# Two attention layers on a graph, fp32: the dense products by one level of Strassen's algorithm

## The chip, the cores and the metric

The kernel runs on one core of a Trainium2 chip, as one launch. The metric is device time in microseconds (us). The engines of the core work side by side, each through its own queue of instructions in order: TensorE (PE in the profile; its weight loads are listed apart as PEld), VectorE (DVE), ScalarE (ACT), GpSimd (POOL), and SyncE (SP), which here only starts transfers.

## The reference

64 graphs of 256 nodes with 512 features pass through two layers of masked attention, each before a residual sum. All arithmetic is fp32.

```python
h = jnp.maximum(_layernorm(x), 0.0)                 # layer 0: 4 heads of 64
q, k, v = h @ Wq, h @ Wk, h @ Wv                    # 512 -> 256
attn = softmax(where(adj, q @ k.T * scale, -max))
x = x + (attn @ v) @ Wo + bo                        # 256 -> 512
h = jnp.maximum(_layernorm(x), 0.0)                 # layer 1: 8 heads of 64
h = layernorm(h) * gamma + beta                     # its own norm on top
q, k, v = split(h @ w_qkv.T)                        # 512 -> 3 x 512
attn = softmax(where(adj | eye, q @ k.T * scale, -1e9))
x = x + (attn @ v) @ w_out.T + b_out                # 512 -> 512
```

## The kernel before, in words

A **step** handles two graphs (G = 2), so 512 tokens; there are 32 steps. Activations of a step lie in SBUF twice: with tokens in the 128 partitions (`xt`, `h`, `v`: four token tiles of 128) and with features in the partitions (`hT`, `oT`: chunks of 128 features by 512 tokens).

Per step and layer the work is:

- **Norm.** Statistics of a token tile on VectorE (`moments`, L140 and L141), the power -1/2 on GpSimd (L145), the scaling of `h` on VectorE (L160 in layer 0, L192 in layer 1). In layer 1 (`norm1_stats`) two norms stand behind each other: centering with the lower bound 0 (L177), statistics again. GpSimd adds the output bias into `xt` (L165 for layer 0, L182 for layer 1).
- **Transposes of h** (`transpose_h`, L204), four chunks; ScalarE (layer 0, with the lower bound 0) or VectorE (layer 1, with gamma and beta) takes them out of PSUM into `hT`.
- **q and k** (`project_qk`): for each pair of heads `pr` (2 pairs in layer 0, 4 in layer 1) and each of q and k, four matmuls of 128 features by 512 tokens (L223); ScalarE copies the result out (L227).
- **V** (`project_v`): for each token tile four matmuls, 256 columns wide in layer 0 and 512 in layer 1 (L235).
- **Attention per pair of heads**: `scores` (called S below: 8 matmuls, L267; then for each of eight 128x256 blocks one VectorE pass with mask and minimum, L276, and one exponential with its sum on ScalarE, L281; then the reciprocal L287 and the multiplication L290 on VectorE), `turn` (T: 16 transposes on TensorE, L304, copied out half by VectorE, L309, half by ScalarE, L311) and `weigh` (W: 8 matmuls with V, L323, copied into `oT` by ScalarE, L328).
- **Output product** (`combine`): for each token tile two (layer 0) or four (layer 1) matmuls of 512 columns (L245); VectorE adds the result into `xt` (L249).

An fp32 matmul appears in the profile as two records, each with its own weight load; a transpose as one.

**What sets the order.** Every call is an event with a time on a nominal clock (`at(period, place, ...)`), and the events are issued sorted by it. Three steps overlap: in one period the kernel does layer 1 of step s, layer 0's attention of step s+1 and layer 0's q, k and V of step s+2. TensorE's order is the written order (`manual_schedule` at L59); the other engines' orders are laid out by the framework's scheduler at build time and are fixed then. PSUM is cut into four buffers for scores and turns (`ps_sc`) and four for everything else (`ps_mm`, the tile name `mm`).

Of the kernel before, what the change touches and what calls it, by code (L numbers as in the profile page):

```python
# [9 lines left out]
U8 = mybir.dt.uint8  # L10
# [9 lines left out]
def kernel(  # L20
# [32 lines left out]
    io = ctx.enter_context(tc.tile_pool(name="io", bufs=3))  # L53
# [20 lines left out]
    wqkv0 = const.tile([P, NC, 3, I0], FP, name="wqkv0")  # L74
    wo0 = const.tile([P, PR0, D], FP, name="wo0")
# [3 lines left out]
    wqkv1 = const.tile([P, NC, 3 * I1], FP, name="wqkv1")  # L79
    wo1 = const.tile([P, PR1, D], FP, name="wo1")  # L80

    def first_weights():
        for k, w in enumerate((wq, wk, wv)):
            nc.scalar.dma_start(wqkv0[:, :, k, :], w.rearrange("(c p) o -> p c o", p=P))
        nc.scalar.dma_start(wo0, wo.rearrange("(c p) o -> p c o", p=P))
        for v, t in ((bo, bo_b), (b_out, bout_b)):
            nc.scalar.dma_start(t, bass.AP(tensor=v.tensor, offset=v.offset, ap=[[0, P], [1, D]]))
# [9 lines left out]
    def weight_loads():  # L97

        blocks = []
        tags = ("h1", "hT1", "qT1", "kT1")  # L100
        for src, dst in ((w_qkv, wqkv1), (w_out, wo1)):
            for r0 in range(0, src.shape[0] // P, 4):
                wr = act.tile([P, 4, src.shape[1]], FP, name="wr", tag=tags[len(blocks)])
                nc.scalar.dma_start(wr, src[r0 * P:(r0 + 4) * P].rearrange("(r p) i -> p r i", p=P))
                blocks.append((wr, dst, r0))
        return blocks

    def weight_block(wr, dst, r0, c):
        pw = ps_mm.tile([P, 4 * P], FP, name="mm")
        for r in range(4):  # L110
            nc.tensor.transpose(pw[:, r * P:(r + 1) * P], wr[:, r, c * P:(c + 1) * P], ident)  # L111
        nc.vector.tensor_copy(dst[:, c, r0 * P:(r0 + 4) * P], pw)
# [4 lines left out]
    def load(s):  # L117
        xt = io.tile([P, NT, D], FP, name="xt", bufs=4)
        nc.sync.dma_start(xt, x[s * G:(s + 1) * G].rearrange("g (t p) d -> p (g t) d", p=P))
        ad = io.tile([P, NT, N], U8, name="ad")  # L120
        nc.sync.dma_start(ad, adj[s * G:(s + 1) * G].rearrange("g (t p) j -> p (g t) j", p=P))
        S[s].update(xt=xt, ad=ad)

    def mask0(s):
        n0 = act.tile([P, NT, N], FP, name="n0")
        nc.gpsimd.tensor_scalar(n0, S[s]["ad"], -1.0, BIG, op0=ALU.add, op1=ALU.mult)
        S[s]["n0"] = n0

    def mask1(s):
        n1 = act.tile([P, NT, N], FP, name="n1")  # L130
        nc.gpsimd.tensor_scalar(n1, S[s]["ad"], -1.0, BIG, op0=ALU.add, op1=ALU.mult)
        for g in range(G):
            v = n1[:, g * NIC:(g + 1) * NIC, :]
            nc.gpsimd.tensor_tensor(v, v, offdiag, ALU.mult)
        S[s]["n1"] = n1
# [12 lines left out]
    def norm0_stats(s):  # L148
        mv = stat.tile([P, NT, 2], FP, name="mv0", bufs=2)
        for t in range(NT):  # L150
            moments(mv, S[s]["xt"], t)
        ve = stat.tile([P, NT], FP, name="ve0", bufs=2)
        nc.vector.tensor_scalar(ve, mv[:, :, 1], EPS, None, op0=ALU.add)
        S[s].update(mv=mv, r=rsqrt(ve, "r0"))

    def norm0_apply(s):
        xt, mv, r = S[s]["xt"], S[s]["mv"], S[s]["r"]
        h = act.tile([P, NT, D], FP, name="h0")
        for t in range(NT):
            nc.vector.tensor_scalar(  # L160
                h[:, t, :], xt[:, t, :], mv[:, t, 0:1], r[:, t:t + 1],
                op0=ALU.subtract, op1=ALU.mult,
            )
        for t in range(NT):
            nc.gpsimd.tensor_tensor(xt[:, t, :], xt[:, t, :], bo_b, ALU.add)  # L165
        S[s]["h"] = h
# [3 lines left out]
    def norm1_stats(s, t):  # L170
        st, x1 = S[s], S[s]["xt"]
        if t == 0:
            st["mv"] = stat.tile([P, NT, 2], FP, name="mv1", bufs=2)
            st["mg"] = stat.tile([P, NT, 2], FP, name="mg", bufs=2)
            st["h"] = act.tile([P, NT, D], FP, name="h1")
        moments(st["mv"], x1, t)
        nc.vector.tensor_scalar(  # L177
            st["h"][:, t, :], x1[:, t, :], st["mv"][:, t, 0:1], 0.0,
            op0=ALU.subtract, op1=ALU.max,
        )  # L180
        moments(st["mg"], st["h"], t)
        nc.gpsimd.tensor_tensor(x1[:, t, :], x1[:, t, :], bout_b, ALU.add)  # L182
        if t == NT - 1:
            ve = stat.tile([P, NT], FP, name="ve1", bufs=2)
            nc.vector.tensor_scalar(ve, st["mv"][:, :, 1], EPS, EPS, op0=ALU.add, op1=ALU.mult)
            nc.vector.tensor_tensor(ve, ve, st["mg"][:, :, 1], ALU.add)
            st["r"] = rsqrt(ve, "r1")

    def norm1_apply(s):
        st = S[s]  # L190
        for t in range(NT):
            nc.vector.tensor_scalar(  # L192
                st["h"][:, t, :], st["h"][:, t, :], st["mg"][:, t, 0:1], st["r"][:, t:t + 1],
                op0=ALU.subtract, op1=ALU.mult,
            )


    def transpose_h(s, lyr, c):
        st = S[s]
        if c == 0:  # L200
            st["hT"] = act.tile([P, NC, T], FP, name=f"hT{lyr}")
        ph = ps_mm.tile([P, T], FP, name="mm")
        for t in range(NT):
            nc.tensor.transpose(ph[:, t * P:(t + 1) * P], st["h"][:, t, c * P:(c + 1) * P], ident)  # L204
        if lyr == 0:
            nc.scalar.activation(st["hT"][:, c, :], ph, AF.Relu)  # L206
        else:
            nc.vector.tensor_scalar(
                st["hT"][:, c, :], ph, gb[:, 0, c:c + 1], gb[:, 1, c:c + 1],
                op0=ALU.mult, op1=ALU.add,  # L210
            )

    def weight(lyr, c, k):
        return wqkv0[:, c, k, :] if lyr == 0 else wqkv1[:, c, k * I1:(k + 1) * I1]

    def project_qk(s, lyr, pr, k):
        st, pairs = S[s], (PR0, PR1)[lyr]
        key = f"{'qk'[k]}T{lyr}"
        if pr == 0:
            st[key] = act.tile([P, pairs, T], FP, name=key)  # L220
        pp = ps_mm.tile([P, T], FP, name="mm")
        for c in range(NC):
            nc.tensor.matmul(  # L223
                pp, weight(lyr, c, k)[:, pr * P:(pr + 1) * P], st["hT"][:, c, :],
                start=(c == 0), stop=(c == NC - 1),
            )
        nc.scalar.copy(st[key][:, pr, :], pp)  # L227

    def project_v(s, lyr, t):
        st, inner = S[s], (I0, I1)[lyr]  # L230
        if t == 0:
            st[f"v{lyr}"] = act.tile([P, NT, inner], FP, name=f"v{lyr}")
        pv = ps_mm.tile([P, T], FP, name="mm")
        for c in range(NC):
            nc.tensor.matmul(  # L235
                pv[:, :inner], st["hT"][:, c, t * P:(t + 1) * P], weight(lyr, c, 2),
                start=(c == 0), stop=(c == NC - 1),
            )
        nc.scalar.copy(st[f"v{lyr}"][:, t, :], pv[:, :inner])  # L239

    def combine(s, lyr, t):
# [192 lines left out]
```

## Time and profile before

| | |
|---|---|
| median of 3 runs (lowest to highest) | 3934.84 us (3934.14 to 3936.08) |
| the profiled execution, time / span | 3935.06 / 3933.3 us |
| granted TensorE clock, mean | 0.998 |
| one step (distance of the same product in two steps) | 121.1 us |
| matmul records on TensorE | 16961 |
| GpSimd busy | 554.5 us, 14% of the span |
| HBM traffic over the span | 20 GB/s |

How to read the profile: the first part gives each engine's busy time and its share of the span. The chain that ended last is followed back from the last instruction, at each step to what released it; it tells whose work sets the end. The groups give, for one line, engine, operation and shape: the count, the busy time and the mean duration in ns of one instruction, then how long the engine stood idle just before them and who ended that. Records of one engine overlap, so the pace of a series is read from starts in the timeline, whose columns are start, time covered, engine, line, operation, shape and count. The waits list who waited for whom: total, times, longest. The table by stretches gives per engine the busy time and the number of instructions, then the granted clock, the share of the DMA engines and GB/s.

### The profile page before, as it was taken

What the parts mean: (1) busy time and instruction counts of PE and PEld (TensorE: products, weight loads), DVE (VectorE), ACT (ScalarE), POOL (GpSimd) and SP (SyncE); (2) the same over time, 40 slices, a digit from 0 to 9 for tenths busy, and PEclk for the clock granted to TensorE, in tenths of its full rate; (3) what the DMA queues carried; (4) which work ended last, traced back from release to release, by engine and by line L of the source; (5) the groups of instructions that cost most, each with busy time, mean ns of one, the idle gap of its engine ahead of it and who ended that gap; (6) DMA issues with size and microseconds to landing.
All of it is one profiled execution on the core that took longest, in us unless ns stands there. A gap on an engine that the chain in (4) does not pass through costs nothing.

```text
span 3933.3 us, 46557 instructions
## 1 busy us (share of the span) xinstructions
PE 3876.5 (99%) x16961; PEld 2178.9 (55%) x16961; DVE 2186.6 (56%) x7025; ACT 1503.9 (38%) x4417; POOL 554.5 (14%) x458
## 2 busy tenths in 40 slices
PE   7999999999999999999999999999999999999999
PEld 4555555555555555555555555555555555555554
DVE  5554655546555456555465554655545655556553
ACT  2434343333343343433434334334334343343333
POOL 3111111011111011111111101111101111111000
PEclk9999999999999999999999999999999999999999
DMA  3000000000000000000000000000000000000000
GB/s 118 1 23 23 23 2 24 22 23 24 2 23 22 23 23 17 9 22 24 23 24 2 23 22 23 24 2 23 22 23 23 13 13 22 23 24 11 1 11 22
DMA packets 55190, 81.10 MB, mean 21 GB/s; under 512 B 18088, under 2 KB 19632, under 8 KB 54960
## 3 DMA queue, kind: packets, MB, share of 16 engines
q1 hardware_dynamic: 50688, 71.31, 5.4%
q10 hardware_dynamic: 4272, 6.82, 0.5%
q8 instruction: 133, 2.18, 0.2%
q14 instruction: 97, 0.79, 0.1%
HBM read 44.57 MB, written 33.55 MB: 20 GB/s over the span
## 4 chain that ended last, share of the span: by engine, by line
PE 98%; ACT 1%; DVE 1%; DMA 0%; issue 0%; ACTq 0%
PE mm L223 34%; PE mm L235 17%; PE mm L245 17%; PE sc L267 9%; PE mm L323 9%; PE sc L304 9%; PE mm L204 3%; ACT kT L227 0%; DMA bout_b<-in_L_gnn_b_out_dram 0%; DVE pm L290 0%; PE mm L111 0%; ACT pm L281 0%; DVE pm L276 0%; DMA xt<-in_x_dram 0%; DVE pT L309 0%
## 5 line engine op out<-in xcount | busy, mean ns | idle before, releaser
L223 PE MATMUL mm<-hT,wqkv 128*128 128x512 f32 x3072 | 1369.2, 595 | 3.3 <-ACT hT L206 3.3
L276 DVE CUSTOM_DVE_ANT_0 pm<-sc,n 128x256 f32<-128x256 f32 x1536 | 544.6, 420 | 989.4 <-PE sc L267 985.7
L223 PEld LDWEIGHTS mm<-hT,wqkv 128*128 128x128 f32 x3072 | 567.2, 190 | 659.5 <-issue 620.7
L281 ACT ACTIVATE pm<-pm,sa 128x256 f32<-128x256 f32 x1536 | 758.5, 495 | 435.6 <-DVE sa L276 435.6
L235 PE MATMUL mm<-wqkv,hT 128*128 128x256 f32 (+1 forms) x2048 | 684.5, 487 | 0.0
L245 PE MATMUL mm<-wo,oT 128*128 128x512 f32 x1536 | 683.3, 594 | 0.0
L290 DVE TENSOR_SCALAR pm<-pm,sa 128x256 f32<-128x256 f32 x1536 | 555.0, 424 | 12.3
L235 PEld LDWEIGHTS mm<-wqkv,hT 128*128 128x128 f32 x2048 | 381.7, 190 | 265.6 <-issue 242.3
L245 PEld LDWEIGHTS mm<-wo,oT 128*128 128x128 f32 x1536 | 281.9, 190 | 319.4 <-issue 311.5
L309 DVE COPY pT<-sc 128x512 f32<-128x512 f32 x384 | 261.1, 687 | 299.2 <-PE sc L304 298.9
L267 PE MATMUL sc<-kT,qT 64*128 64x256 f32 x3072 | 385.6, 390 | 21.6 <-ACT kT L227 21.6
L304 PEld LDWEIGHTS sc<-ident,pm 128*128 128x128 f32 x3072 | 347.6, 142 | 87.2 <-issue 65.3
L304 PE MATMUL sc<-ident,pm 128*128 128x128 f32 x3072 | 372.3, 274 | 12.1 <-DVE pm L290 12.1
L267 PEld LDWEIGHTS sc<-kT,qT 64*128 64x128 f32 x3072 | 282.4, 187 | 179.5 <-issue 105.1
L182 POOL TENSOR_TENSOR xt<-xt,bout_b 128x512 f32<-128x512 f32 x128 | 162.5, 1270 | 1546.0 <-DVE h L177 1507.0
L323 PE MATMUL mm<-pT,v 128*64 128x256 f32 x3072 | 374.5, 386 | 0.0
L227 ACT COPY qT<-mm 128x512 f32<-128x512 f32 x192 | 112.6, 586 | 680.7 <-PE mm L223 680.7
L311 ACT COPY pT<-sc 128x512 f32<-128x512 f32 x384 | 225.2, 586 | 327.0 <-PE sc L304 327.0
L249 DVE TENSOR_TENSOR xt<-mm,xt 128x512 f32<-128x512 f32 x256 | 175.2, 685 | 287.3 <-PE mm L245 287.3
L239 ACT COPY v<-mm 128x256 f32<-128x256 f32 (+1 forms) x256 | 122.6, 479 | 473.7 <-PE mm L235 473.7
L281 ACT ACTIVATION_READ_ACCUMULATOR pm<-pm,sa 128x1 f32 x1536 | 286.4, 186 | 0.0
L227 ACT COPY kT<-mm 128x512 f32<-128x512 f32 x192 | 112.5, 586 | 454.0 <-PE mm L223 454.0
(40 smaller groups left out, 1942.1 us busy)
## 6 DMA issues: line engine op xcount, KB each, us to landing
xt<-in_x_dram SPq DMA_DIRECT2D x32, 1024.0 KB, 5.5
out_dram<-xt SPq DMA_DIRECT2D x32, 1024.0 KB, 4.3
ad<-in_adj_dram SPq DMA_DIRECT2D x32, 128.0 KB, 2.2
wr<-in_L_gnn_w_qkv_dram ACTq DMA_DIRECT2D x3, 1024.0 KB, 13.9
wr<-in_L_gnn_w_out_dram ACTq DMA_DIRECT2D x1, 1024.0 KB, 16.7
wqkv<-in_L_gnn_Wq_dram ACTq DMA_DIRECT2D x1, 512.0 KB, 7.0
wqkv<-in_L_gnn_Wk_dram ACTq DMA_DIRECT2D x1, 512.0 KB
wqkv<-in_L_gnn_Wv_dram ACTq DMA_DIRECT2D x1, 512.0 KB, 12.2
```

The costliest lines, as they stand in the source:

```text
L223: nc.tensor.matmul(pp, weight(lyr, c, k)[:, pr * P:(pr + 1) * P], st["hT"][:, c, :], start=(c == 0), stop=(c == NC - 1),)
L227: nc.scalar.copy(st[key][:, pr, :], pp)
L235: nc.tensor.matmul(pv[:, :inner], st["hT"][:, c, t * P:(t + 1) * P], weight(lyr, c, 2), start=(c == 0), stop=(c == NC - 1),)
L245: nc.tensor.matmul(po[:, :D], st[f"oT{lyr}"][:, pr, t * P:(t + 1) * P], w[:, pr, :], start=(pr == 0), stop=(pr == pairs - 1),)
L267: nc.tensor.matmul(sc[g, e][:, ic, :], qT[rows, pr, i0:i0 + P], kT[rows, pr, g * N:(g + 1) * N], start=True, stop=True,)
L276: nc.vector.tensor_tensor_reduce(out=pm[:, g, e, ic, :], in0=sc[g, e][:, ic, :], in1=neg[:, g * NIC + ic, :], scale=-SCALE, scalar=SMAX, o ...
L281: nc.scalar.activation(pm[:, g, e, ic, :], pm[:, g, e, ic, :], AF.Exp, bias=sa[:, 0, g, e, ic:ic + 1], scale=-1.0, accum_out=sa[:, 1, g, e ...
L290: nc.vector.tensor_scalar(pm[:, g, e, ic, :], pm[:, g, e, ic, :], sa[:, 2, g, e, ic:ic + 1], None, op0=ALU.mult,)
L304: nc.tensor.transpose(pp[:, jc, ic * P:(ic + 1) * P], pm[:, g, e, ic, jc * P:(jc + 1) * P], ident,)
L309: nc.vector.tensor_copy(pT[:, g, e], pp)
L311: nc.scalar.copy(pT[:, g, e], pp)
L323: nc.tensor.matmul(po[e * DH:(e + 1) * DH, g * N:(g + 1) * N], st[f"v{lyr}"][:, g * NIC + jc, c0:c0 + DH], pT[:, g, e, jc, :], start=(jc = ...
```

## The change

Strassen's algorithm multiplies two matrices, each cut into 2 x 2 blocks, with seven block products where the plain way needs eight. The changed kernel applies it (in Winograd's form, with fewer sums) once to each dense product.

- **Blocks.** The features are one cut (halves of the 512 inputs), the two graphs of the step the other. So `hT` and `oT` become tiles of seven blocks [128, 7, chunks, 256 tokens]: four of data, written by the evacuation to the places `B_OF`, and the others made from them by four subtractions on GpSimd (`act_sums`, L94 on), in a chain where most sums need one before. The weights become seven blocks likewise (`weight_sums`, once at the start).
- **Products.** They are issued in the order 1, 6, 7, 5, 2, 4, 3. Products 1, 6, 7 and 5 take a PSUM buffer each; 2, 4 and 3 accumulate onto the buffers of 1, 7 and 5, after those have been read. Product 1 needs data blocks only; product 6 needs the third sum of the chain, 7 the first, 5 the second, 4 the fourth.
- **Sums of results.** For q, k and V (`evacuate`): products 1 and 2 are copied by ScalarE, the other five are added by VectorE to what an earlier product has left in SBUF. For the output product (`accumulate`): VectorE adds six of the seven, GpSimd adds the block u = 1 + 6 into three blocks of `xt`.
- **Shapes.** A product of q and k serves two pairs of heads (one set in layer 0, two in layer 1): 4 matmuls of 256 columns. V has 4 matmuls per product, of 256 columns in layer 1 and 128 in layer 0. The output product has 4 (layer 1) or 2 (layer 0), of 256 columns.
- **Softmax.** The multiplication by the reciprocal moves from VectorE to GpSimd (L407). The turned block goes back into the tile it came from, so `pT` is gone.
- **Norm and loads.** `h` is loaded directly, normed in place and shared by both layers; x is loaded a second time for the residual (`load_x`), with the bias of layer 0 added by GpSimd (L180). `xt` has 2 buffers in place of 4. `norm1` is one event after layer 0's output product.
- **Order.** The nominal clock now counts sets of seven products. A period is: q/k of layer 1, first half; V of layer 1; q/k, second half; layer 0's output product of the next step; q/k of layer 0 and V of layer 0 for the step after that; layer 1's output product. S, T and W of the six pairs are set between them.

The core of the diff (`evacuate`, `accumulate` and the events in full, the rest cut):

```diff
+    A_OF = {(0, 0): 0, (0, 1): 1, (1, 1): 2, (1, 0): 3}
+    B_OF = ((0, 4, 3), (1, 3, 1))
+    PRODUCT = {1: (0, 0), 2: (1, 1), 3: (6, 2), 4: (2, 6), 5: (3, 3), 6: (4, 4), 7: (5, 5)}
...
+    def act_sums(b):
+        eng = nc.gpsimd
+        eng.tensor_tensor(b[:, 5], b[:, 2], b[:, 3], ALU.subtract)
+        eng.tensor_tensor(b[:, 3], b[:, 3], b[:, 0], ALU.subtract)
+        eng.tensor_tensor(b[:, 4], b[:, 2], b[:, 3], ALU.subtract)
+        eng.tensor_tensor(b[:, 6], b[:, 1], b[:, 4], ALU.subtract)
...
+    def norm1(s):
...
+        h = st["h"] = act.tile([P, NT, D], FP, name="h")
+        for t in range(NT):
+            moments(mv, x1, t)
+            nc.vector.tensor_scalar(
+                h[:, t, :], x1[:, t, :], mv[:, t, 0:1], 0.0, op0=ALU.subtract, op1=ALU.max
+            )
+            moments(mg, h, t)
+            nc.gpsimd.tensor_tensor(x1[:, t, :], x1[:, t, :], bout_b, ALU.add)
...
+        scale_rows(h, mg, rsqrt(ve, "r1"))
...
+    def evacuate(n, bank, region):
+        r11, r12, r21, r22 = region
+        add = nc.vector.tensor_tensor
+        if n == 1:
+            nc.scalar.copy(r21, bank)
+        elif n == 6:
+            add(r12, bank, r21, ALU.add)
+        elif n == 7:
+            add(r22, bank, r12, ALU.add)
+        elif n == 5:
+            add(r22, bank, r22, ALU.add)
+        elif n == 2:
+            nc.scalar.copy(r11, bank)
+        elif n == 4:
+            add(r21, bank, r12, ALU.add)
+        else:
+            add(r12, bank, r12, ALU.add)
+
+    def accumulate(n, bank, region, u):
+        r11, r12, r21, r22 = region
+        add = nc.vector.tensor_tensor
+        if n == 1:
+            nc.scalar.copy(u, bank)
+        elif n == 6:
+            add(u, bank, u, ALU.add)
+            nc.gpsimd.tensor_tensor(r12, r12, u, ALU.add)
+            nc.gpsimd.tensor_tensor(r21, r21, u, ALU.add)
+        elif n == 7:
+            add(r22, bank, r22, ALU.add)
+        elif n == 5:
+            add(r22, bank, r22, ALU.add)
+            nc.gpsimd.tensor_tensor(r22, r22, u, ALU.add)
...
+    SHARED = {2: 1, 4: 7, 3: 5}
...
     def project_qk(s, lyr, a, n):
...
+        bank, first = bank_of(st, ("qk", a), n, N)
+        wa, ba = PRODUCT[n]
+        for k in range(2):
+            for c in range(HC):
+                nc.tensor.matmul(
+                    bank[:, k, :], w[:, wa, c, k, a * P:(a + 1) * P], st["hT"][:, ba, c, :],
...
+        evacuate(n, bank, (t0[:, :, :N], t0[:, :, N:], t1[:, :, :N], t1[:, :, N:]))
...
-                    nc.vector.tensor_scalar(
-                        pm[:, g, e, ic, :], pm[:, g, e, ic, :], sa[:, 2, g, e, ic:ic + 1], None,
+                    nc.gpsimd.tensor_scalar(
+                        pm[g, e][:, ic, :], pm[g, e][:, ic, :], sa[:, 2, g, e, ic:ic + 1], None,
...
+    PROD = 1.75
+    SET = 7 * PROD
+    PERIOD = 6 * SET
...
+    def at_set(period, place, share, fn, *args):
+        for i, n in enumerate((1, 6, 7, 5, 2, 4, 3)):
+            at(period, place + i * share / 7, fn, *args, n)
...
+        at(p - 1, 5.6, load_h, s)
+        at(p, 1.0, norm0, s)
+        at(p, 2.9, mask, s, 0)
+        for c in range(NC):
+            at(p, 3.03 + 0.03 * c, transpose_h, s, 0, c)
+        at_set(p, 3.5, 1.0, project_qk, s, 0, 0)
+        at_set(p, 4.5, 0.5, project_v, s, 0)
+        at(p, 4.5, scores, s, 0, 0)
+        at(p, 5.15, turn, s, 0, 0)
+        at(p, 5.6, scores, s, 0, 1)
+        at(p, 5.601, weigh, s, 0, 0, True, False)
+        at(p, 6.3, turn, s, 0, 1)
+        at(p, 7.001, weigh, s, 0, 1, False, True)
+        at(p, 7.5, load_x, s)
+        at_set(p, 9.0, 0.5, combine, s, 0)
+        at(p, 9.5, norm1, s)
...
+        for c in range(NC):
+            at(p, -0.85 + 0.15 * c, transpose_h, s, 1, c)
+        at(p, 0.3, mask, s, 1)
+        at_set(p, 0.0, 1.0, project_qk, s, 1, 0)
+        at_set(p, 1.0, 1.0, project_v, s, 1)
+        at_set(p, 2.0, 1.0, project_qk, s, 1, 1)
+        at(p, 1.0, scores, s, 1, 0)
+        at(p, 1.65, turn, s, 1, 0)
+        at(p, 2.0, scores, s, 1, 2)
+        at(p, 2.001, weigh, s, 1, 0, True, False)
+        at(p, 2.65, turn, s, 1, 2)
+        at(p, 3.0, scores, s, 1, 1)
+        at(p, 3.001, weigh, s, 1, 2, False, False)
+        at(p, 3.5, turn, s, 1, 1)
+        at(p, 3.75, scores, s, 1, 3)
+        at(p, 3.751, weigh, s, 1, 1, False, False)
+        at(p, 4.25, turn, s, 1, 3)
+        at(p, 4.501, weigh, s, 1, 3, False, True)
+        at_set(p, 5.0, 1.0, combine, s, 1)
+        at(p, 6.0, store, s)
```

In the changed file the lines that the prediction names are: L180 the bias of layer 0, L205 the scaling of a norm (`scale_rows`), L270 the add of product 7 in `evacuate`, L322, L344 and L359 the matmuls of q/k, V and the output product, L407 the multiplication by the reciprocal, L419 the transposes of T.

In the order that the scheduler laid out, layer 1's last score block of a step stands between products 6 and 7 of layer 0's q/k on TensorE, and so in the middle of `norm1` on VectorE. There VectorE's order is: the last adds of layer 0's output product, the statistics and centerings of `norm1` with the two copies of T, the add of product 6 and the score passes between them, the scaling L205, the second reciprocal, and then the adds of products 7 and 5. GpSimd's order there is: sums of `hT`, the last add of u, the four additions of the output bias, four multiplications L407, the power of `norm1`, the mask of layer 1 (three operations), four multiplications.

## The prediction, blind

> **What bounds the kernel now.** Read the busy times and the chain that ended last first, then TensorE's waits between 100 and 3800 us.
>
> ```profile
> PE 3876.5 (99%) x16961; PEld 2178.9 (55%) x16961; DVE 2186.6 (56%) x7025; ACT 1503.9 (38%) x4417; POOL 554.5 (14%) x458
> ...
> PE 98%; ACT 1%; DVE 1%; DMA 0%; issue 0%; ACTq 0%
> ```
> ```profile
> PE sc L267 <- ACT kT L227: 21.0, 31, 0.7
> ```
>
> TensorE is the whole path; it waits 0.7 us per step (one step is two batch entries; there are 32). From the chain in order of time, the same product starts at 357.65 and 478.75 us: a step takes 121.1 us, and 3933.3 - 32 x 121.1 = 58 us are fill and drain.
>
> The timeline of TensorE gives paces, start to start (the records overlap):
>
> ```profile
> 2021.05 1.91 PE L304 MATMUL sc<-ident,pm 128*128 128x128 f32 x16
> 2022.80 5.35 PE L235 MATMUL mm<-wqkv,hT 128*128 128x256 f32 x24
> 2028.07 2.00 PE L267 MATMUL sc<-kT,qT 64*128 64x256 f32 x16
> 2030.00 1.95 PE L323 MATMUL mm<-pT,v 128*64 128x256 f32 x16
> ...
> 2061.78 7.03 PE L235 MATMUL mm<-wqkv,hT 128*128 128x512 f32 x16
> 2068.75 2.00 PE L267 MATMUL sc<-kT,qT 64*128 64x256 f32 x16
> ```
>
> A record (two make a matmul; a transpose is one) costs 6.97/16 = 0.436 us at 512 columns, 5.27/24 = 0.220 at 256, 1.75/16 = 0.109 for a 128-column transpose. Halving columns loses nothing. A score block S is 1.93, a weighing W 1.88, a turn T 1.75. Check: 96 q/k records x 0.436, 32 of V x 0.436 and 32 x 0.220, 48 of the output product x 0.436 make 83.6; 6 S + 6 W + 6 T + 8 transposes of h (0.44) make 36.9; with the 0.7 wait 121.2.
>
> **What the change removes from TensorE.** Per step 308 records of 256 columns x 0.220 = 67.6, and V of layer 0, 56 records of 128 columns. The trace has no dense 128-column record. Below, the transposes: 0.109. Above, L235's weight loads take 190 ns each; were they not to overlap, 0.190. I take 0.109, the nearest shape with a new weight per record: 6.1 us (10.6 at the other end). With 36.9, a step without waits is 110.6: 10.5 less than before, 336 us in all.
>
> The Trainium skill, "TensorE: Matmul & The Clock Gate", Back-to-back issue gap, speaks against 0.109: it has 81 ns for 128 columns with a new weight each, against 56 for the stream alone. By that factor, V of layer 0 would cost an estimated 8.8 us, and the sum would rise by 2.7 us a step; no run here shows it yet.
>
> **What it adds elsewhere.** VectorE loses L290 (555 us, 17.3 a step) and L249 (5.5), and gains 32 adds of 128x512 (L249's form, 0.685) and 5 of 128x256: 24. It stays near 69 of 110 us. GpSimd has 17.3 a step and gains 48 multiplications (L290 moved), 16 block sums (12 of 128x512, 4 of 128x256), 6 adds into xt. Its prices:
>
> ```profile
> L182 POOL TENSOR_TENSOR xt<-xt,bout_b 128x512 f32<-128x512 f32 x128 | 162.5, 1270 | 1546.0 <-DVE h L177 1507.0 <-DVE ve L185 39.0
> ...
> L131 POOL TENSOR_SCALAR n<-ad 128x1024 f32<-128x1024 uint8 x32 | 33.6, 1051 | 331.0 <-DVE sa L287 330.9
> ...
> L67 POOL TENSOR_SCALAR offdiag<-ident 128x128 f32<-128x128 f32 x2 | 0.6, 301 | 0.1
> ```
>
> The multiplication is 128x256: above 0.30 (L67), below 0.64 (half an L182); on the line from L67 to L131 it is 0.41, which I take: 19.7. Sums 12 x 1.27 + 4 x 0.65 = 17.8, adds 7.6: GpSimd about 62 of 110 us. ScalarE loses some 4 us of copies. No engine but TensorE is full. So the question is which wait ends last, in the fixed order of the queues. I follow one step of the changed kernel's order; DMA stays far from full (20 GB/s).
>
> *Covered.* Softmax to turn: in the trace the eight exponentials of a score block end 5.6 us after its first matmul; the multiplications then end at 6.2 + 4 x 0.41 = 7.85 us. T follows 9 to 12 us after S in TensorE's order. The nearest are T of layer 0's second pair (GpSimd first has hT's sums and a mask: ready 3.4 into the next step, T at 5.2) and T of layer 1's first pair: the store of the old xt, the second load of x (5.5 us) and GpSimd's four bias adds stand ahead: layer 1's last add waits behind a scaling of norm0 and its power (4.4), so the store is issued about 5.6 us into the step, landed 9.9, load 15.5, adds 20.7, multiplications 24.0, T at 26.3: 2.3 left. SyncE's further loads wait behind that store, but are due most of a step later.
>
> *Output product, layer 0.* Its product 6 needs a PSUM buffer that a W took; ScalarE copies that only after eight exponentials and a copy: **1.2 us** wait (0 if ScalarE is early).
>
> *Output product, layer 1.* Product 6 needs the third block sum of oT1. GpSimd reaches these sums after layer 0's multiplications, 7.9 us after that S, and needs 3 x 1.33: ready 11.9 after S; TensorE arrives at 10.7 (S, W, six narrow products of 0.87, product 1): **1.2 us** (none if V of layer 0 is slow).
>
> *q/k of layer 0: the large one.* Product 4 accumulates onto product 7's bank, so VectorE must first have read product 7. In VectorE's order that add stands behind the whole of norm1, the scores' pass, and norm1's scaling L205, which waits for GpSimd's power. Its prices are in VectorE's timeline:
>
> ```profile
> 2101.68 0.68 DVE L140 BATCH_NORM_STATS2 bs<-h 128x6 f32<-128x512 f32 x1
> 2102.28 0.68 DVE L140 BATCH_NORM_STATS2 bs<-xt 128x6 f32<-128x512 f32 x1
> 2102.88 0.16 DVE L141 BATCH_NORM_AGGREGATE mg<-bs 128x2 f32<-128x6 f32 x1
> 2102.99 0.18 DVE L141 BATCH_NORM_AGGREGATE mv<-bs 128x2 f32<-128x6 f32 x1
> 2103.21 0.49 DVE L177 TENSOR_SCALAR h<-xt,mv 128x512 f32<-128x512 f32 x1
> 2103.73 0.69 DVE L140 BATCH_NORM_STATS2 bs<-h 128x6 f32<-128x512 f32 x1
> ...
> 2109.92 1.92 DVE L192 TENSOR_SCALAR h<-h,mg,r 128x512 f32<-128x512 f32 x4 [0.40 <-POOL r L145]
> ...
> 2121.22 3.82 DVE L160 TENSOR_SCALAR h<-xt,mv,r 128x512 f32<-128x512 f32 x4 [2.26 <-PE mm L204]
> ```
>
> Zero is the end of layer 0's output product. TensorE then has T 1.75, five products of 1.76, S 1.93, W 1.88: it wants product 4 at 14.4. VectorE has, start to start: the last add 0.6, eight statistics 4.8, eight aggregates 1.3, four centerings 1.8, two copies of T 1.2, product 6's add 0.6, seven score passes (0.345 each) 2.4, small ones 0.3: 13.0. It begins 0.6 early, waits 0.4 for T, and two centerings meet GpSimd's sums of hT (about 0.9 each): variance ready at 14.7. GpSimd does four multiplications first (13.8 to 15.4), then the power (1.02): 16.5. L205's four cost 1.9 alone (L192), 3.82 beside GpSimd's adds (L160); here the mask's three operations (1.05, 1.27, 1.27) start with them: 20.3. Then a reciprocal 0.2, the add 0.6, a hop 0.1: 21.2. TensorE waits **6.8 us**. Without any collision and at 0.30 per multiplication the chain ends at 17.6: 3.2; with the two operations strictly taking turns and 0.64: 9.3.
>
> The Trainium skill, "SBUF — State Buffer", SBUF: two separate sides, calls the port pair of VectorE and GpSimd an exclusive lock. L160's third and fourth taking 1.49 us where an undisturbed one takes 0.55 agrees; by strict turns the scaling would cost 1.05 + 2 x 1.27 + 4 x 0.46 = 5.4 instead of 3.82, and the wait 8.4.
>
> *Clock.* Idle TensorE loses its clock:
>
> ```profile
> 48.00:56.00 8.00, 5.84 (x28) 4.52 (x30) 4.90 (x21) 3.58 (x12) 0.00 (x0) 0.65 0.00 1
> ```
>
> The granted clock was 0.65 here after a gap of 2.5 us, and the S in it took 3.7 instead of 1.93. I add **1.8 us** per large wait.
>
> **Sum.** 110.6 + 1.2 + 1.2 + 6.8 + 1.8 = 121.6 a step, against 121.1: nearly all the gain is given back. Fill and drain: 58, plus sums ahead of lone products 9, last turns without cover 8, clock 3.6: about 20 (0 to 60). 32 x 121.6 + 78 = 3969. The profiled execution took 3935.06 us with a span of 3933.3, so 1.8 lie around it (its time is 0.2 above the median of the runs, 3934.84): 3971, say **3970 us**.
>
> **Rivals.**
> - *GpSimd late, narrow products slow* (slower still): 0.64 per multiplication and 0.190 per narrow record. Step 121.6 + 0.9 + 4.5 - 1.2 = 125.8, x 32 + 80: 4105. For it: GpSimd goes from 14% to over half, and its queue is in order. Against: transposes at 0.109.
> - *The wait is short* (faster): collisions nearly free, power early; it decides once product 7's add comes under 5 us late. 110.6 + 3.2 + 1.8 + 0.6 + 0.5 = 116.7: 3815. Against: VectorE's own 13 us of work in a 14.4 us stretch.
> - *The gain is kept*: no wait. 32 x 110.6 + 80 = 3619. It needs another order on VectorE than the one built.
>
> **Chances.** Forecast 0.52 (own range 3900 to 4050; of it 0.10 faster, 0.07 same, 0.35 slower), GpSimd late 0.24, short wait 0.17, gain kept 0.07. Within 0.2% (what a measurement can tell from no change) is 3927 to 3943. Faster 0.34, same 0.07, slower 0.59. Bounds: low ends 3794 (step 116.7, fill as before), high ends (9.3 of wait, 2.5 of clock, 0.190) 128.1 x 32 + 118 = 4217; the range 3800 to 4200 leaves out the kept gain and the outermost tails.
>
> **What would show it.** TensorE's waits should name VectorE's add of product 7 (L270) at L322, 31 or 32 times, 5 to 9 us each, with a lower granted clock behind; L359 waiting for GpSimd about 1 us; L407 near 0.41 us; L344 near 0.109 us start to start. The forecast is wrong if L322 hardly waits, if turns (L419) wait for GpSimd, or if the narrow records are load-bound.

## The result, and the profile after

The changed kernel takes **4386.18 us** (median of 4 runs, 4378.62 to 4395.02), the kernel before 3934.49 beside it: a ratio of 1.1148 (95% interval 1.1127 to 1.117). The direction was the one held likeliest; the size was not, and 4386 lies beyond the range of 3800 to 4200. The profiled execution has a span of 4385.7 us and a mean granted clock of 0.951. Layer 0's power (L200 on GpSimd) starts at 554.87 us and, 24 steps later, at 3783.78 us: a step takes 134.54 us on average (133.1 to 136.7), where 121.6 were predicted.

The page's busy times, the chain that ended last, and the group of the moved multiplication:

```profile
PE 3774.3 (86%) x21953; PEld 3076.2 (70%) x21953; DVE 2282.2 (52%) x6425; ACT 1379.1 (31%) x4177; POOL 2763.4 (63%) x2706
...
PE 40%; POOL 32%; DVE 15%; DMA 5%; issue 4%; ACT 3%; POOLq 0%; ACTq 0%; DVEq 0%; SPq 0%
...
L407 POOL TENSOR_SCALAR pm<-pm,sa 128x256 f32<-128x256 f32 x1536 | 1388.2, 924 | 893.7 <-DVE sa L404 608.5
```

TensorE fell from 99% to 86% busy, and the chain, which was TensorE's alone, now runs over GpSimd for a third of the span, though GpSimd is idle 37% of it. The third line says why: one multiplication took **0.92 us** (0.90 start to start), where the prediction took 0.41. No other new group is off by such a factor: GpSimd's sums of 128x512 took 1.26 to 1.30 (1.27 expected).

TensorE's waits between 300 and 4100 us (engine and line, what was waited for, then us in total, times, longest); there are 28 steps in it:

```profile
PE mm L322 <- DVE qk L270: 242.1, 28, 8.9
PE mm L359 <- POOL oT L98: 98.0, 28, 3.5
PE mm L322 <- DVE xt L300: 45.8, 28, 1.6
PE sc L419 <- POOL pm L407: 38.0, 73, 0.6
PE mm L322 <- POOL hT L98: 28.7, 28, 1.0
PE mm L359 <- ACT oT L443: 21.7, 28, 0.8
PE mm L344 <- ACT oT L443: 11.2, 28, 0.4
```

The first is the wait that the prediction put first: product 4 of layer 0's q/k, for VectorE's add of product 7. It is 8.6 us a step, in every step. The second, for the third block sum of `oT`, is three times the predicted 1.2. Four of the seven were not in the sum at all. Together: 485.5 / 28 = 17.3 us a step.

How the first comes about, in the timelines of TensorE, GpSimd and VectorE (start, us, engine, line):

```profile
2116.14 3.75 PE L322 MATMUL mm<-hT,wqkv 128*128 128x256 f32 x8 [8.64 <-DVE qk L270]
```
```profile
2106.04 3.62 POOL L407 TENSOR_SCALAR pm<-pm,sa 128x256 f32<-128x256 f32 x4
2109.63 1.04 POOL L200 TENSOR_TENSOR r<-ve,mhalf 128x4 f32<-128x4 f32 x1
```
```profile
2092.37 0.69 DVE L298 TENSOR_TENSOR xt<-mm,xt 128x512 f32<-128x512 f32 x1 [1.55 <-POOL xt L289]
...
2093.70 0.67 DVE L300 TENSOR_TENSOR xt<-mm,xt 128x512 f32<-128x512 f32 x1
...
2110.70 4.63 DVE L205 TENSOR_SCALAR h<-h,mg,r 128x512 f32<-128x512 f32 x4 [3.75 <-POOL r L200]
2115.34 0.65 DVE L270 TENSOR_TENSOR qk<-mm,qk 128x512 f32<-128x512 f32 x1
```

In VectorE's timeline the variance (L235) comes at 2106.45, which is 14.8 us after layer 0's output product ended (14.7 was predicted). Then it stands 3.75 us before L205, since GpSimd has just begun four multiplications of 3.62 us and only then takes the power. The four scalings take 4.63 us beside the mask, and the add of product 7 comes last. The eight records after the wait took 3.75 us in place of 1.97: in the windows view the clock was 0.77 from 2106 to 2116 us and 0.54 from 2116 to 2122.

### The profile page after: what moved, and what is told of

Its sections match the earlier page's. It is cut to its first block, busy times and chain, and to the rows that moved or that the text cites. A ratio compares the mean times of both kernels' runs of the same rounds, so it can differ in the third digit from the quotient of the medians.

```text
span 4385.7 us, 60584 instructions
## 1 busy us (share of the span) xinstructions
PE 3774.3 (86%) x21953; PEld 3076.2 (70%) x21953; DVE 2282.2 (52%) x6425; ACT 1379.1 (31%) x4177; POOL 2763.4 (63%) x2706
## 4 chain that ended last, share of the span: by engine, by line
PE 40%; POOL 32%; DVE 15%; DMA 5%; issue 4%; ACT 3%; POOLq 0%; ACTq 0%; DVEq 0%; SPq 0%
POOL pm L407 19%; PE mm L322 16%; PE mm L359 7%; PE sc L419 5%; PE mm L344 4%; PE sc L383 4%; DVE h L205 3%; ACT pm L399 3%; DVE bs L195 3%; PE mm L437 3%; DMA xt<-in_x_dram 2%; POOL xt L180 2%; DVE h L228 2%; DMA out_dram<-xt 2%; POOL r L200 1%
## 5 line engine op out<-in xcount | busy, mean ns | idle before, releaser
L407 POOL TENSOR_SCALAR pm<-pm,sa 128x256 f32<-128x256 f32 x1536 | 1388.2, 924 | 893.7 <-DVE sa L404 608.5
L322 PE MATMUL mm<-hT,wqkv 128*128 128x256 f32 x5376 | 1286.7, 395 | 357.0 <-DVE qk L270 259.4
L322 PEld LDWEIGHTS mm<-hT,wqkv 128*128 128x128 f32 x5376 | 1038.9, 197 | 552.8 <-issue 297.8
L359 PE MATMUL mm<-wo,oT 128*128 128x256 f32 x2688 | 666.2, 395 | 144.0 <-POOL oT L98 120.6
L359 PEld LDWEIGHTS mm<-wo,oT 128*128 128x128 f32 x2688 | 500.0, 194 | 254.2 <-POOL oT L98 133.7
L344 PE MATMUL mm<-wqkv,hT 128*128 128x128 f32 (+1 forms) x3584 | 627.5, 330 | 12.0 <-ACT oT L443 12.0
L344 PEld LDWEIGHTS mm<-wqkv,hT 128*128 128x128 f32 x3584 | 545.1, 191 | 86.8 <-issue 24.5
L425 ACT COPY pm<-sc 128x512 f32<-128x512 f32 x384 | 224.8, 585 | 1076.9 <-PE sc L419 1021.1
L419 PE MATMUL sc<-ident,pm 128*128 128x128 f32 x3072 | 428.2, 288 | 66.5 <-POOL pm L407 62.9
L419 PEld LDWEIGHTS sc<-ident,pm 128*128 128x128 f32 x3072 | 378.1, 150 | 120.9 <-POOL pm L407 100.1
L383 PE MATMUL sc<-qk 64*128 64x256 f32 x3072 | 387.3, 391 | 3.8 <-DVE pm L423 3.7
L437 PE MATMUL mm<-pm,v 128*64 128x256 f32 x3072 | 377.5, 388 | 0.0
L180 POOL TENSOR_TENSOR xt<-xt,bo_b 128x512 f32<-128x512 f32 x128 | 161.9, 1297 | 331.0 <-DMA xt<-in_x_dram 294.4
L383 PEld LDWEIGHTS sc<-qk 64*128 64x128 f32 x3072 | 280.6, 188 | 84.9 <-issue 47.3
L423 DVE COPY pm<-sc 128x512 f32<-128x512 f32 x384 | 257.6, 687 | 156.5 <-PE sc L419 146.6
L205 DVE TENSOR_SCALAR h<-h,mg,r 128x512 f32<-128x512 f32 x128 | 143.1, 1177 | 115.2 <-POOL r L200 115.2
```

Of the source, the lines that this page charges most:

```text
L205: nc.vector.tensor_scalar(h[:, t, :], h[:, t, :], mean[:, t, 0:1], r[:, t:t + 1], op0=ALU.subtract, op1=ALU.mult,)
L322: nc.tensor.matmul(bank[:, k, :], w[:, wa, c, k, a * P:(a + 1) * P], st["hT"][:, ba, c, :], start=first and (k, c) == (0, 0), stop=(k, c) ...
L344: nc.tensor.matmul(bank[:, t, :], st["hT"][:, ba, c, t * P:(t + 1) * P], w[:, wa, c, 2, :], start=first and (t, c) == (0, 0), stop=(t, c) ...
L359: nc.tensor.matmul(bank[:, t, :], st[f"oT{lyr}"][:, ba, c, t * P:(t + 1) * P], w[:, wa, c, :], start=first and (t, c) == (0, 0), stop=(t, ...
L383: nc.tensor.matmul(sc[g, e][:, ic, :], qk[rows, 0, i0:i0 + P], qk[rows, 1, g * N:(g + 1) * N], start=True, stop=True,)
L407: nc.gpsimd.tensor_scalar(pm[g, e][:, ic, :], pm[g, e][:, ic, :], sa[:, 2, g, e, ic:ic + 1], None, op0=ALU.mult,)
```

## The experiments

Theory: GpSimd's multiplication is so long that norm1's chain, the sums of `oT` and the turns wait for it. Rivals: norm1's place in VectorE's queue alone; contention of GpSimd and VectorE whoever multiplies. All ratios are against the kernel before, with 95% intervals.

### Who multiplies, and where norm1 stands

**mult_on_vector**: L407 from `nc.gpsimd.tensor_scalar` to `nc.vector.tensor_scalar`.

> The changed kernel with the multiplication L407 back on VectorE, all else as it is. Theory A (GpSimd's multiplication takes 0.90 us start to start where 0.41 was reckoned, and all that stands behind it in GpSimd's queue is late): the waits of L359 for GpSimd's sums of oT (3.5 us a step), of L419 for L407 (1.0) and of the first product for L300 (1.6) go; the wait of L322 for L270 stays, since VectorE has two of the multiplications more in front of the add: ve ready 15.2 us after layer 0's output product, power 16.3, L205 20.9, add done 22.8, wanted at 14.4, so 8.4 us. Step 110.6 + 1.2 + 8.4 + 2.8 of clock + 0.6 = 123.6, time about 4035 us. Rival B (the narrow products themselves run slower than reckoned): above 4250 us, since nothing on TensorE changes.

4021.12 us, ratio 1.0217 (1.0202 to 1.0233): 365 us back. The waits for `oT` L98, `hT` L98 and the turns are gone; L322 still waits 4.2 us a step for L270, with norm1 ahead of it, and V of layer 0 now waits 2.0 for its adds behind multiplications on VectorE.

**norm1_late**: the changed kernel, norm1 a set later.

```diff
-        at(p, 9.5, norm1, s)
+        at(p, 10.45, norm1, s)
```

> The changed kernel with norm1 issued after layer 0's q/k products (place 10.45 for 9.5), so that VectorE's add of product 7 stands ahead of the power and of L205; GpSimd keeps the multiplication. Theory A: the wait of L322 for L270 shrinks from 8.6 to about 1 us, but the turn behind it then waits for GpSimd: four multiplications 14.4 to 18.0 us after layer 0's output product, parts of the mask and a bias add to 21.6, four more to 25.2, where the turn wants the last at 17.5. About 7 us of wait stay under another name (L419 for L407), time 4280 to 4390 us. Rival C (VectorE's order alone makes the wait): the 8.6 us and the 2.8 of clock go, step 121.7, time about 3975 us.

4330.38 us, 1.1006 (1.099 to 1.1023). The wait for L270 is gone (0.4 us in all, 300 to 3900 us), and yet only 56 us came back, 1.8 a step. The turns now wait 126 us for L407, up to 2.2 us each, and the sums of `oT` are 3.5 late as before: waits fell only from 17.3 to 13.2 us a step, and what TensorE does between them got slower: the step less its waits is 132.9 - 13.2 = 119.7 us, where the changed kernel has 117.2. More of the cold clock falls on work: of 28 steps, the eight records after the wait for `oT` took 1.99 us in four and 3.7 or more in 16, in the changed kernel 1.99 in ten and 3.7 or more in two. Behind the largest wait stood the same late engine.

**vector_and_late**: both edits.

> Both edits: multiplication on VectorE and norm1 behind layer 0's q/k. Theory A with VectorE's order as second cause: neither engine holds product 4 up for long: VectorE's add of product 7 is done about 16 to 17 us after layer 0's output product, wanted at 14.4. Step 110.6 + 1.2 + 2 + 0.5 + 0.6 = 115, time 3700 to 3800 us, faster than the kernel before. Rival B (narrow products slow): above 3935 us.

A miss: 4016.31 us, 1.02 (1.0183 to 1.0217). L322 waits 4.4 us for L270 again, though norm1's power and scaling no longer stand ahead of it (part of its statistics and centerings still does). VectorE's timeline: four multiplications elsewhere, then the first four that the add of product 7 (at 2064.92) stands behind:

```profile
2021.75 1.14 DVE L407 TENSOR_SCALAR pm<-pm,sa 128x256 f32<-128x256 f32 x4
...
2058.09 4.02 DVE L407 TENSOR_SCALAR pm<-pm,sa 128x256 f32<-128x256 f32 x4
```

Four take 1.14 us alone and 4.02 while GpSimd makes layer 1's mask (L185 and L189, from 2058.26 to 2061.96).

**vector_late_one_mask** tests that: both edits, layer 1's mask made in the first step only.

```diff
     def mask(s, lyr):
+        if lyr == 1 and s > 0:
+            S[s]["n1"] = S[0]["n1"]
+            return
```

> Both edits of vector_and_late (multiplication on VectorE, norm1 at 10.45), and layer 1's mask made once, for the first step, and used for all: this leaves out 31 of 32 masks of layer 1, three operations of GpSimd each. Theory A: the 4.4 us that product 4 still waits in vector_and_late come from VectorE's multiplications being held up by that mask (four took 4.02 us beside it, 1.14 elsewhere). Without it 2.9 us of the wait go, and about 1 us of cold clock: L322 waits for L270 1 to 2 us, the step is 118 to 119, the time 3870 to 3920 us. Rival: the wait is the length of VectorE's own queue ahead of L270 (seven score passes, eight multiplications, a reciprocal that waits for ScalarE); it stays above 3.5 us and the time above 3980.

3904.75 us, 0.9919 (0.9904 to 0.9934); L322 waits 44.8 / 29 = 1.5 us. The first four multiplications ahead of the add (L410 in this file, at 2119.75) take 1.14 us, as alone. As theory A said: the mask was it.

**before_mult_on_gpsimd**: the kernel before, its multiplication L290 alone on GpSimd.

> The kernel before with nothing but L290 moved to GpSimd. Theory A says that the price is one of place in GpSimd's queue: here the queue is nearly empty, eight multiplications end 4.2 + 8 x 0.90 = 11.4 us after the scores begin, the turns want the last block 10.4 to 15.5 us after; so 1 to 2 us a step, 3960 to 4000 us, with L290 at about 0.92 us on GpSimd. Rival D (the multiplication on GpSimd slows any kernel by its own length): 8 us and more a step, above 4190 us.

4048.56 us, 1.029 (1.0274 to 1.0305), between the two expectations: 113 us more without any Strassen product. The step grew from 121.1 to 123.7 us, 2.6, of which 1.7 (49.4 us in 29 steps) is turns waiting for L290; the other 30 us are fill and drain. GpSimd has little else to do there; so the multiplication is dear by itself (942 ns for one), and dearer in a queue with sums, where moving it back to VectorE gained 365 us.

### What the multiplication costs, by form

**mult_as_two_tensors**: still on GpSimd, the reciprocal broadcast along the row.

```diff
-                    nc.gpsimd.tensor_scalar(
-                        pm[g, e][:, ic, :], pm[g, e][:, ic, :], sa[:, 2, g, e, ic:ic + 1], None,
-                        op0=ALU.mult,
+                    nc.gpsimd.tensor_tensor(
+                        pm[g, e][:, ic, :], pm[g, e][:, ic, :],
+                        sa[:, 2, g, e, ic:ic + 1].to_broadcast([P, N]), ALU.mult,
```

> The multiplication L407 stays on GpSimd, but as an operation on two tensors (the reciprocal broadcast along the row) in place of one on a tensor and a value per partition. Theory A: the 0.92 us is the price of the form with a value per partition; two tensors of 128x256 took 0.73 us in the block sums, so 0.19 less each. On the path stand the four ahead of the power (0.8 us), the eight ahead of the third sum of oT1 (1.5) and some of the small waits (0.5): 2.8 us a step, 4386 - 32 x 2.8 = about 4296 us (4270 to 4330), and L407 reads 0.70 to 0.76 us. Rival: GpSimd pays for a broadcast operand or for work beside VectorE whatever the form; L407 stays above 0.85 us and the time within 4370 to 4410.

4058.47 us, 1.0311 (1.0295 to 1.0326): **328 us** from the form alone, far more than the 90 expected. GpSimd's timeline at the place shown above:

```profile
2074.32 2.33 POOL L407 TENSOR_TENSOR pm<-pm,sa 128x256 f32<-128x256 f32 x4
```

2.33 / 4 = 0.58 us, less than the sums' 0.73, and two thirds of 0.90. Theory A was right in kind; the price was lower still, and the eight in a row ahead of the sums of `oT` took 4.61 in place of 7.21 us, so that wait fell from 3.5 to 0.9.

**no_mult**: no multiplication at all (the attention is left unnormalized).

> The changed kernel without the multiplication L407 at all, which leaves the weights of the attention unnormalized; norm1 where the changed kernel has it. Theory A: norm1's chain alone (VectorE's 13 us, the power, the scaling beside the mask) keeps 4 to 5 us of wait at product 4, and 1.5 of cold clock: step 119 to 122, 3870 to 3980 us. Rival: the wait was the multiplications on GpSimd alone; L322 waits under 2 us and the time is under 3820 us.

3946.34 us, 1.0028 (1.0017 to 1.004); L322 waits for L270 5.75 us. So the multiplication makes 4386 - 3946 = 440 us of the time, 13.7 us a step, and norm1's chain without it keeps its own wait.

**no_mult_late**: that, and norm1 at 10.45.

> As no_mult (no multiplication L407, so the attention is unnormalized), and norm1 at 10.45. It shows what is to be had when the multiplication costs nothing anywhere. Theory A: all large waits go; left are ScalarE's copy of W (0.8 to 1.2) and small ones, step 113.5 to 115.5, 3700 to 3780 us. Rival: block sums, VectorE's longer queue and the cold clock cost 5 us a step without any multiplication: over 3840 us.

**3753.72 us**, 0.954 (0.9524 to 0.9556), clock 0.996. Here the seven products show their gain. Without the multiplication norm1's later place is worth 3946.34 - 3753.72 = 193 us; with it on GpSimd (norm1_late) it was worth 56. Waits left, of 29 steps:

```profile
PE mm L322 <- DVE qk L270: 52.0, 29, 1.8
PE mm L359 <- ACT oT L437: 23.4, 29, 0.8
```

**vector_two_tensors_late**: as vector_and_late, in the two-tensor form.

> As vector_and_late (multiplication on VectorE, norm1 at 10.45), but the multiplication as an operation on two tensors, the reciprocal broadcast. Theory A: what GpSimd's mask held up in vector_and_late is the form with one tensor and a value per partition; an operation on two tensors is not held up, so that four L407 beside the mask take at most 2.2 us (vector_and_late 4.02) though one costs more alone (about 0.35 against 0.29): L322 waits for L270 1.5 to 3 us, 3890 to 3960 us. Rival: any operation of VectorE that reads and writes the same SBUF beside GpSimd is held up; L407 takes over 3.5 us for four there and the time is 4000 to 4040 us.

4092.09 us, 1.0401 (1.0383 to 1.0418): the rival's mechanism, and slower than it said. Four take 1.43 us alone on VectorE and 4.41 beside the mask; this form is held up as well.

### A place for it

**mult_on_scalar** (an activation with a scale per partition, `nc.scalar.mul`) and **scalar_and_late** (that, with norm1 at 10.45).

> The multiplication L407 alone moved from GpSimd to ScalarE (an activation with a scale per partition), norm1 where the changed kernel has it. Theory A: GpSimd's lateness goes (oT1's sums, hT's sums, turns), ScalarE has room (31% busy, 48 x 0.37 to 0.5 us more a step), and product 4 of layer 0 still waits for norm1's chain without GpSimd's multiplications ahead of the power: 5 us, with 2 of cold clock, and ScalarE's later copies of W 1.5 to 2: step 120 to 122, time 3890 to 4000 us. Rival: ScalarE's queue becomes the late one; L359 waits for ScalarE's oT copy over 3 us and the time is over 4040.

4117.56 us, 1.0465 (1.0447 to 1.0482). The rival held: L359 waits 4.0 us a step for ScalarE's copy of W, which now stands behind multiplications, and L322 4.7 us.

> The multiplication on ScalarE and norm1 at 10.45. Theory A: neither GpSimd nor norm1 nor a collision of VectorE with GpSimd's mask is ahead of L270 any more; left are ScalarE's copies of W (1.5 us), L270 and L300 behind a filler of VectorE (1 us) and clock (0.5): step 113 to 115, 3680 to 3780 us, below the kernel before. Rival: VectorE's queue ahead of L270 (seven passes, the reciprocal behind ScalarE's exponentials, two centerings) keeps 3 us or more of wait at product 4: over 3830 us.

3929.83 us, 0.9984 (0.9975 to 0.9993): neither. L322 is down to 1.3 us a step, but the 4.0 at L359 stay, where 1.5 were expected.

**two_tensors_and_late**: the two-tensor form on GpSimd, norm1 at 10.45.

> The multiplication on GpSimd as an operation on two tensors (0.58 us start to start in mult_as_two_tensors, against 0.90 as it stands in the changed kernel) and norm1 at 10.45. Theory A: the 7.4 us a step that L322 waited for L270 in mult_as_two_tensors and the cold clock behind it (1.5 to 2) go, and nothing as large takes their place, since VectorE has no multiplications in its queue (unlike vector_and_late) and ScalarE's copies of W come as early as in the changed kernel (unlike scalar_and_late, 4.0 us): 4058 - 32 x 9 = about 3770 us (3700 to 3820), below the kernel before. Rival: GpSimd is late for the turns, as in norm1_late (L419 waited 126 us for L407), and the oT sums keep over 1 us: over 3850 us.

A miss: 3963.82 us, 1.0072 (1.0057 to 1.0087). L322 waits 0.3 us a step, the turns 1.0; but the scores L383 wait 3.5 us for VectorE's copy of a turn (L423), since VectorE stands at L205 until GpSimd, behind multiplications, mask and bias adds, has taken the power. The wait had moved one product on.

**mult_shared_late**: each score block's first graph on GpSimd (two tensors), its second on ScalarE; norm1 at 10.45.

> The multiplication shared: the first graph's four on GpSimd as operations on two tensors, the second graph's four on ScalarE; norm1 at 10.45. Theory A: each engine's queue is short enough; ScalarE's copies of W come 2 us earlier than in scalar_and_late (L359 waits for oT 1 to 2 us in place of 4.0), GpSimd's power comes 2 us earlier than in two_tensors_and_late (L383 waits for L423 under 2 us in place of 3.5): step 116 to 118.5, 3780 to 3860 us, below the kernel before. Rival: in the two runs named, waits of 5.7 to 6.3 us a step stood in a step 9 to 10 us over TensorE's own work; if many small waits and the clock behind them hold it, 3890 to 3960 us.

3913.18 us, 0.9946 (0.9931 to 0.9961), clock 0.976: the rival's range. Its two large waits (a third, L322 for L270, is 4.5 us in all):

```profile
PE sc L383 <- DVE pm L428: 87.6, 28, 3.1
PE mm L359 <- ACT oT L448: 64.6, 28, 2.3
```

**shared_scale_apart**: norm1's scaling as an event of its own at 10.95.

> As mult_shared_late, with norm1's last part, the scaling L205, as a step of its own at 10.95, so that it stands further back in VectorE's queue. Theory A: what is left of waits is VectorE standing at L205 until GpSimd's power is done, with the copies of a turn behind it; 1 to 2 us a step go, so 30 to 60 us less than mult_shared_late. Rival: no change by more than 15 us, since the copy still stands behind one of the scalings.

3911.23 us, 0.9942 (0.9928 to 0.9957), both waits as before: the rival. The event's later place did not put the copy ahead of L205 in VectorE's queue.

**mult_by_pair**: as mult_shared_late, but each of its two waits gets the multiplication out of the queue that causes it.

```diff
-                    if g == 0:
+                    if (g == 0 or (lyr, pr) == (1, 1)) and (lyr, pr) != (1, 3):
                         nc.gpsimd.tensor_tensor(
```

> As mult_shared_late, but for two of layer 1's four pairs the multiplication is not shared: all eight on GpSimd (two tensors) for the pair whose score block stands ahead of layer 0's output product (so that ScalarE copies the W ahead of it earlier), all eight on ScalarE for the pair whose score block stands in layer 0's q/k products (so that GpSimd reaches the mask, the last bias add and norm1's power 2.4 us earlier). Theory A: the two waits left in mult_shared_late are these two queues (L383 behind L423's copy and L205 behind the power, 3.1 us; L359 behind ScalarE's copy, 2.3), and the cold clock after them: 3.9 us a step of wait and 1.5 to 2 of clock go: 3913 - 32 x 5.6 = about 3735 us (3710 to 3790). Rival: other waits come up behind them, or the clock stays at 0.976: 3830 to 3920 us.

**3785.38 us**, 0.962 (0.9607 to 0.9633; lowest to highest 3782.8 to 3786.04). It is faster than both kernels, and lies in theory A's range, 50 us above its sum. Its step is 2152.14 - 2036.95 = 115.2 us, its clock 0.995, and its page and waits (29 steps) read:

```profile
PE 3621.3 (96%) x21953; PEld 2996.6 (79%) x21953; DVE 2292.3 (61%) x6425; ACT 1683.0 (45%) x4945; POOL 1817.7 (48%) x1938
```
```profile
PE mm L322 <- DVE sa L404: 52.0, 29, 1.8
PE mm L359 <- ACT oT L448: 20.8, 29, 0.7
PE sc L383 <- ACT v L266: 12.1, 29, 0.4
```

TensorE does the same 21953 records as in the changed kernel, 600 us sooner. Against mult_shared_late, waits fell by 5.6 - 2.9 = 2.7 us a step, and the time by 128 us, 4.0 a step. The rest, 1.3, fits the clock in kind: from 0.976 to 0.995, 1.9% of a step of 119.5 us, would be 2.3.

## Why the prediction was wrong

The step that failed is one term: "on the line from L67 to L131 it is 0.41, which I take". L407 measured 0.90 us start to start. The line ran through a small and a large operation whose scalars are constants; L407 takes a value per partition from a tensor. Its upper bound, 0.64, was half an operation on two tensors. That is near the two-tensor forms (0.58 to 0.61 with the reciprocal broadcast, 0.73 for a difference), but the form in the kernel costs more than either. The bound was no bound, for no row had this form on GpSimd; and as 48 stand in a step, 0.49 us each was 24 us of GpSimd's time. That the form is the cause is shown by mult_as_two_tensors; no run tries a constant scalar in fp32 at this size, so what in the form is dear stays open.

Term by term, us a step:

| | predicted | measured |
|---|---|---|
| TensorE's own work | 110.6 | 112.3 (mult_by_pair: 115.2 less its waits of 2.9) |
| product 4 of layer 0's q/k | 6.8 | 8.6 |
| third sum of `oT`, layer 1 | 1.2 | 3.5 |
| W's buffer, layer 0 | 1.2 | 0.8 |
| turns; `hT` sums; L300; V | 0 | 1.4; 1.0; 1.6; 0.4 |
| cold clock | 1.8 | 4.9 (what is left) |
| step | 121.6 | 134.5 |

Fill and drain came to 4385.7 - 32 x 134.54 = 80 us against 78: that term was right, and nearly all of the miss lies in the steps (32 x 12.9 = 413 us).

- *Right: the mechanism; one of its numbers by luck.* L322 names L270 in every step. The variance was ready at 14.8 for 14.7, but errors cancel in it. VectorE's last add (L300) was to begin 0.6 us before the output product's end and began 2.0 after it, since the add ahead of it (L298) waits 1.55 us in every step for GpSimd's add of u (L289), which stands behind multiplications; in no_mult it waits 0.2. The work from there took 2.6 us less than reckoned; 1.0 of that is the two centerings beside GpSimd's sums, entered with some 1.9 us, which cost 0.95 (0.85 and 1.06 us for 0.48). Then the four multiplications took 3.6 us for 1.6 and the scaling 4.6 for 3.8, so that the add of product 7 was done at 24.3 (21.2 predicted), and product 4 was wanted at 15.8 (14.4). Without the multiplication the chain's own wait was 5.75 (no_mult); the prediction's sum less its four multiplications gives 6.8 - 1.6 = 5.2.
- *Wrong through the same term: the cover.* Turns were to have 1.8 and 2.3 us left, and the sums of `oT` to be 1.2 late, with eight multiplications at 3.3 us. They took 7.2, and the cover was gone at every place where GpSimd's queue meets TensorE; norm1_late, without the large wait, still stood at 1.10. The prediction had named turns that wait for GpSimd as a sign of being wrong, and they do wait (L419, 73 times). The wait for L300 has the same source: the prediction had that add late behind a power, but counted only the store behind it, not the q/k product. That power now stands behind eight multiplications, and in VectorE's timeline the scaling ahead of the add waits for it:

```profile
2033.89 0.55 DVE L205 TENSOR_SCALAR h<-h,mv,r 128x512 f32<-128x512 f32 x1 [6.76 <-POOL r L200]
```

- *Right: the narrow records.* V of layer 0 took 3.68 / 32 = 0.115 us a record (0.109 taken). The rule of the Trainium skill's "TensorE: Matmul & The Clock Gate", Back-to-back issue gap, weighed in the prediction (8.8 us for V, an estimate), is not borne out by these fp32 records: 56 of them are 6.4 us.
- *Right in direction: collisions.* L205 x4 took 4.63 beside the mask for 3.82, and on VectorE four multiplications 4.02 for 1.14. The 4.63 lies between the row (3.82) and the strict turns of the Trainium skill's "SBUF — State Buffer", SBUF: two separate sides (5.4, an estimate). That page counts VectorE's operations with two SBUF inputs among those that are held up, and vector_two_tensors_late agrees (4.41 for 1.43).
- *Rivals.* "GpSimd late" had the right engine and, at 4105, still too low a price. "The gain is kept" (3619) asked for another order; no_mult_late (without the multiplication) and mult_by_pair, with other orders, come to 3754 and 3785.

Had L407 cost 0.41, the time would lie between no_mult (3946) and mult_as_two_tensors (4058); on the line between them 4026, an estimate, so some 55 us of the 416 missing are other terms; TensorE's own work alone, 1.7 us a step, makes 54. Of the 1.7, the narrow records are 0.3.

What stays open: where the rest of the 1.7 comes from, and whether a step under 115 us can be ordered with the multiplication in it (no_mult_late, without it, is at 114.8).

## What to carry to other kernels

Price a moved operation by a row of the same engine *and the same kinds of operands*; where the trace has none, the range must reach well past the nearest rows, and the first experiment is that operation in another form. An engine at 63% can be the bound: what counts is what stands ahead of the instruction that someone waits for, so take an operation out of the one queue where it is late (mult_by_pair) rather than out of all. When the largest wait goes and the time stays, look for the same late engine at the next place.

## What the runs showed of the hardware

- On GpSimd, 128x256 in fp32: 0.90 us start to start with a value per partition (one tensor), 0.58 with the same value broadcast as a second tensor, 0.73 for a difference of two tensors. On VectorE, without GpSimd beside it, 0.29 and 0.36. The Trainium skill's "GPSIMD Engine Reference", 4.1 Engine selection, has two-input operations about twice slower on GpSimd than on VectorE and one-input ones near line rate; here the two-tensor form is 1.6 times slower than on VectorE (0.58 to 0.36), and the one-input form with a value per partition 3.1 times (0.90 to 0.29).
- The same wait did not always cost the same clock. After waits of 1.8 us the pace stayed as it was in all 29 steps of mult_by_pair (8 records 1.97 us), but before V of layer 0 in mult_on_vector, where a wait of 4.2 us stands earlier in the step, eight narrow records took 1.16 us in 11 steps and 1.8 to 2.0 in 13. After 2.3 us in mult_shared_late four records took 1.13 in 16 steps and 1.5 to 2.1 in 14; after 3.1 us sixteen took 2.24 in 13 steps, 2.65 in six and 3.5 to 3.8 in ten (2.00 undisturbed); after 4.0 us in mult_on_scalar four took 2.04 in all 29. So a wait of 2.3 us or more could cost up to 1.8 us beyond its length in the records just behind it.
